# Fourteen weight pieces of the second convolution move from GpSimd in the scan to VectorE beside two attentions

## The chip, the cores and the metric

The kernel runs on one core of a Trainium2 chip. The metric is the device time of one execution in microseconds; times are compared as medians of several runs, profiles show one execution. Engines: PE (TensorE, matmuls), DVE (VectorE), ACT (ScalarE), POOL (GpSimd) and SP, whose queue issues most of the DMA transfers.

## The reference

Two layers work on x of shape (4, 512, 32, 32), float32. Both take a group norm of their input and add their result to it.

```python
# layer 0: a selective state-space scan over L = 1024 tokens, d_inner = 1024, 16 states
xz = layernorm(tokens) @ W_in                     # xm, z
xs = silu(causal_conv4(xm))
proj = xs @ W_x                                   # dt (32), B (16), C (16)
dt = softplus(proj[:, :32] @ W_dt + b_dt)
h = exp(dt * A) * h + dt * x * B                  # per channel and state
y = sum_s(h * C) + xs * D
out = (y * silu(z)) @ W_out
# layer 1: position attention between two 3x3 convolutions
sp = softmax(center(x)^T top(x))                  # 1024 x 1024, over all its elements
x2 = x + sp @ conv3x3(x, w_bottom)
out = conv3x3(x2, w_out)
```

## The kernel before

Layer 0. Work is cut into units (b, e, h, s): image b (4, called batch here), a pair e of 128-channel blocks (4), a half h of the tokens (2) and a state s (16), so 128 units per image and 512 in all. In a unit, ACT makes exp(dt*A) (line 837), DVE scans twice (line 889), and the product with C and the sum over s follow. The product of dt*x with B is made in one of two ways, by the table B_ON_ACT: on ACT, which scales transposed rows (line 849, four instructions of 128x256), with PE transposing them back (line 875, eight 128x128 transposes); or on POOL (line 864, one instruction of 128x1024 with B broadcast by a DMA). The product with C is one POOL instruction of 128x1024 (line 911), or two of 128x512 on DVE (line 905) for the states in C_ON_DVE. PE sums over s by transposing matmuls (line 918).

The convolutions of layer 1 are Winograd convolutions, four rows by two columns of output at a time: six row taps by four column taps. Their transformed weights are computed in layer 0, in 16 pieces for each convolution (`transform`, line 1159 on): three loads of 192 KB, two scalings on ACT (lines 1177 and 1178), three additions of 128x768 (1185, 1191, 1195) and nine of 128x256 (1203 to 1205) on POOL, and twelve stores to DRAM, to ub (first convolution, w_bottom) or uo (second, w_out). All 32 pieces are steps that fill gaps.

The order of layer 0 is written out by a planner, `Plan`: each step has an engine, an expected duration and a priority (units counted along the scan), and of the steps that can start the one with the smallest priority goes first, within a window. Piece k has the priority -5 for the first 7 (t0) and then tg * (k - 7).

Layer 1. Per image: `scores` (PE: pt and psc, ACT copies them to the eight tiles st, DVE takes the maximum, ACT the exponential), `conv3` (24 loads of 1 MB of weights, uw, each for four matmuls of 128x512 into one PSUM tile m; DVE forms the input transforms rr and v and the outputs n and y, POOL helps), `attend` (eight groups of matmuls pat, each evicted by one DVE instruction into the image, line 1566) and a second `conv3`, whose result `finish` transposes back, adds to the loaded residual and stores. `norm` normalizes the next image. The order before is, for each image b: conv b, attention b, scores b+1, second conv o, finish. In the last image the second convolution's first input is computed chunk by chunk within the attention (`by_chunk`), and half of the transposes back come before the last matmuls (`last`).

In layer 1 the recording framework orders the instructions of each engine and frees buffers of a tag as their readers end. Tag v (16 KB per partition) has two buffers, for the v tiles and for x1t, the image that norm reads; tag u three, for the convolution's weights; PSUM pool ps three.

Of the kernel before, what the change touches and what calls it, by code (L numbers as in the profile page):

```python
# [8 lines left out]
F32 = mybir.dt.float32  # L9
AF = mybir.ActivationFunctionType  # L10
ALU = mybir.AluOpType
# [16 lines left out]
GS = 16  # L28


PRM = dict(pg=0.53, kt=2, ke=1, ka=-0.68, fl=0, fi=4.6, m0=48, n0=50.77, nl=2.05, c0=61.67, cg=6.03, p0=112, e0=6, eg=4.75, g0=78.98, gg=9.04, o0=13.03, og=5.23, dl=8.5, t0=7, tg=18.5, zl=11.5, f1=1.5)


class Buf:
# [137 lines left out]
def mamba_then_pab_kernel(  # L172
# [70 lines left out]

    NP6, NQ = 6, 4
    ub, uo = (
        [
            dram.tile([NP6, P, NCC, C], F32, tag=f"u_{n}_{q}", name=f"u_{n}_{q}")
# [30 lines left out]
    with ExitStack() as l0:  # L280
# [1014 lines left out]
    with ExitStack() as l1:  # L1295
# [104 lines left out]

        shape = [P, NCC, TI, WW + 2]

        def by_chunk(name, xg):

            e, f = (
                tp.tile(shape, F32, tag="rt", name=f"{n}_{name}", bufs=4) for n in "ef"
            )
            r = tp.tile([P, 2, *shape[1:]], F32, tag="rr", name=f"rr_{name}_1", bufs=1)
            v = xp.tile([P, NQ, 2, NCC, P], F32, tag="v", name=f"v_{name}_1", bufs=2)

            def chunk(c):
                rows = [xg[:, c, a : a + 4 * TI - 3 : 4, :] for a in range(5)]
                for t, a in ((e, 2), (f, 1)):
                    nc.scalar.activation(t[:, c], rows[a], AF.Copy, scale=-4.0)
                    nc.gpsimd.tensor_add(t[:, c], t[:, c], rows[a + 2])
                nc.vector.tensor_add(r[:, 0, c], e[:, c], f[:, c])
                nc.vector.tensor_sub(r[:, 1, c], e[:, c], f[:, c])
                x = [r[:, :, c, :, a : a + 2 * TJ - 1 : 2] for a in range(4)]
                vq = [
                    v[:, q, :, c].rearrange("p n (i j) -> p n i j", j=TJ) for q in range(NQ)  # L1420
                ]
                nc.vector.tensor_sub(vq[2], x[2], x[1])  # L1422
                nc.vector.tensor_add(vq[1], x[1], x[2])
                nc.vector.tensor_sub(vq[0], x[0], x[2])
                nc.vector.tensor_sub(vq[3], x[1], x[3])

            return v, chunk

        def conv3(name, xg, u, bias, first=None, late=None):

# [3 lines left out]
            def rows(a):  # L1434
                return xg[:, :, a : a + 4 * TI - 3 : 4, :]

            def tmp(n):
                return tp.tile(shape, F32, tag="rt", name=f"{n}_{name}", bufs=4)

            def flat(t):  # L1440
                return t.rearrange("p c i x -> p (c i x)")

            def inputs(pair):

                r = tp.tile([P, 2, *shape[1:]], F32, tag="rr", name=f"rr_{name}_{pair[0]}", bufs=1)
                r0, r1 = r[:, 0], r[:, 1]
                if pair == (1, 2):
                    e, f = tmp("e"), tmp("f")
                    nc.scalar.activation(e, rows(2), AF.Copy, scale=-4.0)
                    nc.scalar.activation(f, rows(1), AF.Copy, scale=-4.0)  # L1450
                    nc.gpsimd.tensor_add(e, e, rows(4))
                    nc.gpsimd.tensor_add(f, f, rows(3))
                    nc.vector.tensor_add(r0, e, f)
                    nc.vector.tensor_sub(r1, e, f)
                    return r
                if pair == (3, 4):
                    g, h = tmp("g"), tmp("h")
# [9 lines left out]
                k, l = tmp("k"), tmp("l")  # L1467
# [8 lines left out]
            kept = []  # L1476
            y = [None] * 4
            for pair in PAIRS:
                if first and pair == (1, 2):
                    v = first  # L1480
                else:
                    r = inputs(pair)

                    v = xp.tile([P, NQ, 2, NCC, P], F32, tag="v", name=f"v_{name}_{pair[0]}", bufs=2)
                    rv = r.rearrange("p n c i x -> p (n c i) x")
                    x = [rv[:, :, a : a + 2 * TJ - 1 : 2] for a in range(4)]
                    vq = [v[:, q].rearrange("p n c (i j) -> p (n c i) j", j=TJ) for q in range(NQ)]
                    nc.vector.tensor_sub(vq[2], x[2], x[1])
                    nc.vector.tensor_add(vq[1], x[1], x[2])
                    nc.vector.tensor_sub(vq[0], x[0], x[2])  # L1490
                    nc.vector.tensor_sub(vq[3], x[1], x[3])
                ns = []
                for k, p in enumerate(pair):
                    m = {}
# [51 lines left out]
        def attend(b, xg, st, rp, xb, between, chunk):  # L1546


            for k in range(NCC * NH):
# [48 lines left out]
        def finish(b, y):  # L1598

            for j in range(NCC):  # L1600
                o = load_sum(b, j, fp, "f4")
                for rr in range(2):
                    turn_back(b, j, o, y, rr)
                nc.scalar.dma_start(dst[b][:, j, :], o)
# [14 lines left out]
        xg = image[0]  # L1619
        st, rp = scores(0, xg)  # L1620
        for b in range(B):
            xb = conv3(f"b{b}", xg, ub, brow[0])
            after = norm(b + 1) if b + 1 < B else iter(())
            next(after, None)

            v, chunk = by_chunk(f"o{b}", xg) if b + 1 == B else (None, None)
            attend(b, xg, st, rp, xb, after, chunk)
            if b + 1 == B:
                last(b, xg, v)
                break  # L1630
            st, rp = scores(b + 1, image[b + 1])
            finish(b, conv3(f"o{b}", xg, uo, brow[1]))
            xg = image.get(b + 1)


# [55 lines left out]
```

## Time and profile before

| | us |
|---|---|
| median of 3 runs (3073.21 to 3087.27) | 3081.69 |
| the profiled execution | 3079.09 |
| its span | 3077.3 |
| busy PE | 2789.0 (91%) |
| busy DVE | 2290.1 (74%) |
| busy ACT | 1822.0 (59%) |
| busy POOL | 2125.4 (69%) |
| layer 0, by the trace | about 0 to 2045 |
| layer 1 | about 2045 to 3077 |

The first table of the profile page counts busy time over the whole span, which mixes two layers of very different work; the views by stretch, given further on, hold them apart. In a group of instructions the columns are: line, engine, operation, output and inputs with shapes and count, then busy time and mean ns of one, then the idle time just before them and what ended it. Busy time of PE counts overlapped matmuls once, so busy time over count can be smaller than the mean.

### The profile page before, as it was taken

The page shows a single profiled execution, that of the slowest core. Times are in us where ns is not written, and L with a number is a line of the kernel's source. Part 1 is how long each engine was busy: PE and PEld are TensorE (multiplying, and loading weights), DVE is VectorE, ACT ScalarE, POOL GpSimd, SP SyncE. Part 2 cuts the span into 40 slices and gives each one's busy share as a digit, 9 for nine tenths or more (in the row PEclk, how much of TensorE's full clock was granted, in tenths as well). Part 3 has the DMA queues.
Part 4 walks back from the last instruction along what each step waited for, and adds up shares of the span by engine and source line. Part 5 has one row for each costly group of instructions (what it writes and reads, how often), then busy time and mean ns, then how long its engine had stood idle before and what let it go on. Part 6 is the DMA issues. An engine that isn't in the chain of part 4 may idle for free.

```text
span 3077.3 us, 36921 instructions
## 1 busy us (share of the span) xinstructions
PE 2789.0 (91%) x11896; PEld 1669.4 (54%) x11896; DVE 2290.1 (74%) x2989; ACT 1822.0 (59%) x3300; POOL 2125.4 (69%) x1197
## 2 busy tenths in 40 slices
PE   6788789999889999888999968879999999999998
PEld 2556566566666666666666656644444444444444
DVE  4579999888999988989988879985285375346344
ACT  4679878898888888788898879941120030030000
POOL 6989888899978899978889999952151143134222
PEclk9899899999999999999999989999999999999999
DMA  6756455577645577745567654448178458628827
GB/s 183 219 171 210 142 158 155 174 233 241 210 139 173 179 222 239 237 128 162 164 189 222 213 159 140 134 121 319 43 266 316 155 175 317 245 85 312 302 86 260
DMA packets 404537, 600.07 MB, mean 195 GB/s; under 512 B 47192, under 2 KB 246104, under 8 KB 379768
## 3 DMA queue, kind: packets, MB, share of 16 engines
q1 hardware_dynamic: 395536, 583.18, 59.8%
q10 hardware_dynamic: 8648, 14.26, 1.3%
q8 instruction: 95, 1.56, 0.2%
q14 instruction: 98, 0.80, 0.1%
q0 software_dynamic: 160, 0.26, 0.0%
HBM read 500.60 MB, written 96.99 MB: 194 GB/s over the span
## 4 chain that ended last, share of the span: by engine, by line
PE 40%; DVE 12%; ACT 6%; DMA 4%; POOL 4%; issue 3%; SPq 0%; DVEq 0%; POOLq 0%; ACTq 0%
PE m_o L1503 10%; PE m_b L1503 8%; PE pat L1553 7%; DVE da L889 5%; PE y L918 3%; PE po L402 2%; PE psc L1380 2%; PE u L875 2%; DMA uw_b<-u_b 2%; POOL da L911 2%; DVE dbx L889 2%; DVE u L889 1%; PE pz L402 1%; PE pp L728 1%; ACT sc L849 1%
## 5 line engine op out<-in xcount | busy, mean ns | idle before, releaser
L911 POOL TENSOR_TENSOR da<-da,cbc 128x1024 f32<-128x1024 f32 x328 | 773.2, 2368 | 114.7 <-DVE da L889 53.1
L849 ACT ACTIVATE sc<-dtxt,bt_sb 128x256 f32<-128x256 f32 x1312 | 578.1, 499 | 99.3 <-PE u L875 98.5
L837 ACT ACTIVATE da<-dt,a_sb 128x512 f32<-128x512 f32 x656 | 454.1, 716 | 78.8 <-PE y L918 62.8
L864 POOL TENSOR_TENSOR dbx<-dtx,bbc 128x1024 f32<-128x1024 f32 x184 | 434.4, 2373 | 10.6 <-DVE carry_sb L894 4.6
L889 DVE TENSOR_TENSOR_SCAN da<-da,carry_sb,u 128x512 f32<-128x512 f32 x328 | 403.1, 1262 | 42.4 <-PE u L875 40.1
L918 PE MATMUL y<-ident,da 128*128 128x128 f32 x2624 | 366.6, 284 | 72.1 <-POOL da L911 69.9
L889 DVE TENSOR_TENSOR_SCAN da<-da,u 128x512 f32<-128x512 f32 x328 | 397.9, 1213 | 31.0 <-PE u L875 29.0
L875 PE MATMUL u<-ident,sc 128*128 128x128 f32 x2624 | 389.2, 282 | 23.5 <-DVE da L889 14.8
L918 PEld LDWEIGHTS y<-ident,da 128*128 128x128 f32 x2624 | 309.4, 146 | 180.6 <-POOL da L911 132.3
L875 PEld LDWEIGHTS u<-ident,sc 128*128 128x128 f32 x2624 | 314.2, 145 | 113.5 <-issue 34.2
L1503 PE MATMUL m_b<-uw_b,v_b 128*128 128x512 f32 x768 | 337.6, 596 | 17.5 <-issue 8.3
L1503 PE MATMUL m_o<-uw_o,v_o 128*128 128x512 f32 x768 | 334.1, 595 | 4.5 <-DVE v_o L1422 4.1
L402 PE MATMUL pxm<-xt,winc 128*128 128x341 f32 (+4 forms) x768 | 251.0, 470 | 21.7 <-DVE xs L661 10.5
L1503 PEld LDWEIGHTS m_b<-uw_b,v_b 128*128 128x128 f32 x768 | 143.4, 190 | 204.1 <-issue 187.1
L402 PE MATMUL pz<-xt,winc 128*128 128x512 f32 x512 | 244.8, 599 | 8.8 <-DMA winc<-in_w_in_dram 2.5
L837 ACT ACTIVATE u<-dt,a_sb 128x512 f32<-128x512 f32 x368 | 245.5, 681 | 11.9 <-DVE da L889 6.7
L1503 PEld LDWEIGHTS m_o<-uw_o,v_o 128*128 128x128 f32 x768 | 145.6, 191 | 190.2 <-issue 181.7
L918 PE MATMUL y<-ident,dbx 128*128 128x128 f32 x1472 | 215.4, 285 | 36.0 <-DVE dbx L905 24.7
L918 PEld LDWEIGHTS y<-ident,dbx 128*128 128x128 f32 x1472 | 175.7, 147 | 88.2 <-DVE dbx L905 25.8
L1553 PE MATMUL pat<-y_b,st 128*128 128x512 f32 x512 | 221.7, 593 | 0.1
L661 DVE SCALAR_TENSOR_TENSOR xs<-pxm,cw_sb,xs 128x341 f32<-128x341 f32 (+8 forms) x288 | 163.6, 569 | 60.6 <-ACT xs L652 53.6
L1511 ACT ACTIVATE e_b<-m_b 128x512 f32<-128x512 f32 x24 | 14.3, 596 | 316.4 <-PE m_b L1503 300.0
(220 smaller groups left out, 4315.4 us busy)
## 6 DMA issues: line engine op xcount, KB each, us to landing
cbc<-bcd SPq DMA_DIRECT2D x512, 256.0 KB, 3.6
uw_b<-u_b SPq DMA_DIRECT2D x96, 1024.0 KB, 5.1
uw_o<-u_o SPq DMA_DIRECT2D x96, 1024.0 KB, 4.9
bbc<-bcd SPq DMA_DIRECT2D x184, 256.0 KB, 3.9
u_b<-work SPq DMA_DIRECT2D x192, 128.0 KB, 3.0
u_o<-work SPq DMA_DIRECT2D x192, 128.0 KB, 3.4
winc<-in_w_in_dram SPq DMA_DIRECT2D x72, 256.0 KB, 3.7
szd<-sz SPq DMA_DIRECT2D x32, 512.0 KB, 4.0
```

The costliest lines, as they stand in the source:

```text
L402: lambda k=k, lhs=lhs, rhs=rhs: nc.tensor.matmul(p()[:, at : at + cols], lhs(), rhs(), start=(k == 0), stop=(k == n - 1)),
L661: nc.vector.scalar_tensor_tensor(u()[:, first:end], p()[:, first - k - at + before : n - k + before], cw[k], u()[:, first:end], ALU.mult, ...
L837: nc.scalar.activation(t, dt()[:, j], AF.Exp, scale=a_sb[:, at : at + 1])
L849: nc.scalar.activation(sc()[:, k], dtxt()[:, k], AF.Copy, scale=bt[:, at, s : s + 1])
L864: lambda: nc.gpsimd.tensor_mul(hc(), dtx(), b_bc().to_broadcast([P, 2, T])),
L875: nc.tensor.transpose(u()[:, k * P : (k + 1) * P], sc()[:, k, j, :], ident)
L889: nc.vector.tensor_tensor_scan(ht, *((hc()[:, j], u()) if on_act else (u(), hc()[:, j])), carry_sb[:, j, s : s + 1] if h else 0.0, ALU.mul ...
L911: lambda: nc.gpsimd.tensor_mul(hc(), hc(), c_bc().to_broadcast([P, 2, T])),
L918: nc.tensor.matmul(y[j]()[:, k, :], hc()[:, j, k * P : (k + 1) * P], ident, start=(s == 0 and k == 0), stop=(s == NS - 1 and k == NK - 1), ...
L1380: nc.tensor.matmul(pt, top[:, m * P : (m + 1) * P], center[:, h * T : (h + 1) * T], start=True, stop=True,)
L1503: nc.tensor.matmul(m[q], v[:, q, k, c, :], w[:, c, :], start=(c == 0), stop=(c == NCC - 1 and not extra),)
L1553: nc.tensor.matmul(pt, st[m][:, 2 * P * j + h : 2 * P * (j + 1) : 2], xb[m // 2][:, m % 2, :], start=(m == 0), stop=(m == NMC - 1),)
```

## The change

Sixteen pieces of the first convolution's weights and two of the second's stay in layer 0 on POOL (EARLY = 2; tg 42 instead of 18.5). The other fourteen pieces are made by a new function `piece`, on DVE, seven beside the attention of image 0 and seven beside that of image 1. A piece has three loads, six DVE instructions on 384 elements, three on 768, and four stores of 128x6x128. The images go in pairs, so that both attentions of the first pair come before any second convolution: conv b0, attention 0, scores 1, conv b1, attention 1, conv o0, conv o1, scores 2, conv b2, and so on. norm(2) is called inside conv o1. The first input of conv o of a pair is computed before the pair's second attention (`first_inputs`); `by_chunk` goes. The tile of a piece has the tag v, its result the tag u.

In layer 0, nine of sixteen B products are on ACT instead of ten (ten instead of eleven in the last batch), and in the last batch three C products are on DVE instead of two.

```diff
-PRM = dict(pg=0.53, ..., t0=7, tg=18.5, zl=11.5, f1=1.5)
+PRM = dict(pg=0.53, ..., t0=7, tg=42, zl=11.5, f1=1.5)
...
-    NP6, NQ = 6, 4
+    NP6, NQ, EARLY = 6, 4, 2
...
-        B_ON_ACT = [(0, 2, 4, 6, 7, 8, 10, 12, 14, 15)] * (B - 1) + [(0, 2, 3, 4, 6, 8, 10, 11, 12, 14, 15)]
-        C_ON_DVE = [(1, 5, 9, 13)] * (B - 1) + [(5, 13)]
+        B_ON_ACT = [(0, 2, 4, 6, 8, 10, 12, 14, 15)] * (B - 1) + [(0, 2, 4, 6, 7, 8, 10, 12, 14, 15)]
+        C_ON_DVE = [(1, 5, 9, 13)] * (B - 1) + [(3, 9, 13)]
...
-        for k in range(2 * NPC):
+        for k in range(NPC + EARLY):
             u, src = ((ub, w_bottom), (uo, w_out))[k // NPC]
             transform(u, src, k % NPC, -5 if k < PRM['t0'] else PRM['tg'] * (k - PRM['t0']))
...
+        def first_inputs(name, xg):
+            r = row_pair(name, 1)
+            ts = []
+            for n, a in (("e", 2), ("f", 1)):
+                t = tmp(n, name)
+                rows = [xg[:, :, k : k + 4 * TI - 3 : 4, :] for k in (a, a + 2)]
+                nc.scalar.activation(t, rows[0], AF.Copy, scale=-4.0)
+                nc.gpsimd.tensor_add(t, t, rows[1])
+                ts.append(t)
+            nc.vector.tensor_add(r[:, 0], *ts)
+            nc.vector.tensor_sub(r[:, 1], *ts)
+            return spread(name, 1, r)
+
+        def piece(k):
+            c, part = divmod(k, C // QC)
+            cs = slice(part * QC, (part + 1) * QC)
+            taps = w_out[c * P : (c + 1) * P, :, cs].rearrange("p (y x) o -> p y x o", y=3)
+            t = xp.tile([P, NQ, 2, NCC, P], F32, tag="v", name=f"w_{k}", bufs=2)
...
+            nc.sync.dma_start(g[:, 0], taps[:, 0])
+            nc.sync.dma_start(g[:, NP6 - 1], taps[:, 2])
+            nc.sync.dma_start(mid[:, 0], taps[:, 1])
...
+            dve.tensor_add(r[1], r[0], r[5])
+            stt(r[3], r[5], 4.0, r[0], ALU.mult, ALU.add)
+            dve.tensor_sub(r[2], r[1], m)
+            dve.tensor_add(r[1], r[1], m)
+            stt(r[4], m, -2.0, r[3], ALU.mult, ALU.add)
+            stt(r[3], m, 2.0, r[3], ALU.mult, ALU.add)
+            o = fp.tile([P, NCC, C], F32, tag="u", name=f"wo_{k}", bufs=3)
...
+            dve.tensor_add(o[:, 0], g[:, :, 0], g[:, :, 2])
+            dve.tensor_sub(o[:, 1], o[:, 0], g[:, :, 1])
+            dve.tensor_add(o[:, 0], o[:, 0], g[:, :, 1])
+            for q, part in enumerate((g[:, :, 0], o[:, 0], o[:, 1], g[:, :, 2])):
+                nc.sync.dma_start(uo[q].rearrange("n p c o -> p n c o")[:, :, c, cs], part)
...
-                if h and chunk:
-                    chunk(j)
+                for job in also[k : k + 1]:
+                    if job is not None:
+                        piece(job)
...
+        left = list(range(EARLY, NPC))
+        half = len(left) // 2
+        st, rp = scores(0, image[0])
+        for a in range(0, B, 2):
+            for b in (a, a + 1):
+                xb = conv3(f"b{b}", image[b], ub, brow[0])
+                also = [None] * (8 - half) + left[b * half : (b + 1) * half] if not a else []
+                after, v = iter(()), None
+                if b == a:
+                    after = norm(b + 1)
+                    next(after)
+                else:
+                    v = first_inputs(f"o{a}", image[a])
+                attend(b, image[b], st, rp, xb, after, also)
+                if b == a:
+                    st, rp = scores(b + 1, image[b + 1])
+            finish(a, conv3(f"o{a}", image[a], uo, brow[1], v))
+            if a + 2 == B:
+                last(a + 1, image[a + 1], None)
+                break
+            y = conv3(f"o{a + 1}", image[a + 1], uo, brow[1], mid=lambda: normed(a + 2))
+            finish(a + 1, y)
+            st, rp = scores(a + 2, image[a + 2])
```

More of the change, by code (lines that the diff above doesn't have):

```diff
@@ L28 @@
 GS = 16
-PRM = dict(pg=0.53, kt=2, ke=1, ka=-0.68, fl=0, fi=4.6, m0=48, n0=50.77, nl=2.05, c0=61.67, cg=6.03, p0=112, e0=6, eg=4.75, g0=78.98, gg=9.04, o0=13.03, og=5.23, dl=8.5, t0=7, tg=18.5, zl=11.5, f1=1.5)
+PRM = dict(pg=0.53, kt=2, ke=1, ka=-0.68, fl=0, fi=4.6, m0=48, n0=50.77, nl=2.05, c0=61.67, cg=6.03, p0=112, e0=6, eg=4.75, g0=78.98, gg=9.04, o0=13.03, og=5.23, dl=8.5, t0=7, tg=42, zl=11.5, f1=1.5)
 class Buf:
@@ L1401, in mamba_then_pab_kernel @@
         shape = [P, NCC, TI, WW + 2]
[L1403 to L1427, printed above, removed]
@@ L1429, in conv3, with spread @@
-        def conv3(name, xg, u, bias, first=None, late=None):
+        def spread(name, p, r):
+            v = xp.tile([P, NQ, 2, NCC, P], F32, tag="v", name=f"v_{name}_{p}", bufs=2)
+            rv = r.rearrange("p n c i x -> p (n c i) x")
+            x = [rv[:, :, a : a + 2 * TJ - 1 : 2] for a in range(4)]
+            vq = [v[:, q].rearrange("p n c (i j) -> p (n c i) j", j=TJ) for q in range(NQ)]
+            nc.vector.tensor_sub(vq[2], x[2], x[1])
+            nc.vector.tensor_add(vq[1], x[1], x[2])
+            nc.vector.tensor_sub(vq[0], x[0], x[2])
+            nc.vector.tensor_sub(vq[3], x[1], x[3])
+            return v
@@ new lines, in tmp, with row_pair @@
+        def tmp(n, name):
+            return tp.tile(shape, F32, tag="rt", name=f"{n}_{name}", bufs=4)
+        def row_pair(name, p):
+            return tp.tile([P, 2, *shape[1:]], F32, tag="rr", name=f"rr_{name}_{p}", bufs=1)
+        def first_inputs(name, xg):
[10 more added lines that the diff above has]
+            return spread(name, 1, r)
@@ new lines, in piece @@
+        def piece(k):
[3 more added lines that the diff above has]
+            t = xp.tile([P, NQ, 2, NCC, P], F32, tag="v", name=f"w_{k}", bufs=2)
+            t = t.rearrange("p q n c t -> p (q n c t)").rearrange("p (r o) -> p r o", o=QC)
+            g, mid = (t[:, a : a + n].rearrange("p (r x) o -> p r x o", x=3) for a, n in ((0, 3 * NP6), (3 * NP6, 3)))
+            nc.sync.dma_start(g[:, 0], taps[:, 0])
+            nc.sync.dma_start(g[:, NP6 - 1], taps[:, 2])
+            nc.sync.dma_start(mid[:, 0], taps[:, 1])
+            r = [g[:, n].rearrange("p x o -> p (x o)") for n in range(NP6)]
+            m = mid[:, 0].rearrange("p x o -> p (x o)")
+            stt, dve = nc.vector.scalar_tensor_tensor, nc.vector
+            dve.tensor_add(r[1], r[0], r[5])
[5 more added lines that the diff above has]
+            o = fp.tile([P, NCC, C], F32, tag="u", name=f"wo_{k}", bufs=3)
+            o = o.rearrange("p c o -> p (c o)").rearrange("p (q r o) -> p q r o", o=QC, r=8)[:, :, :NP6]
+            dve.tensor_add(o[:, 0], g[:, :, 0], g[:, :, 2])
[3 more added lines that the diff above has]
+                nc.sync.dma_start(uo[q].rearrange("n p c o -> p n c o")[:, :, c, cs], part)
@@ L1434, in rows, with conv3 @@
+        def conv3(name, xg, u, bias, first=None, late=None, mid=None):
             def rows(a):
                 return xg[:, :, a : a + 4 * TI - 3 : 4, :]
-            def tmp(n):
-                return tp.tile(shape, F32, tag="rt", name=f"{n}_{name}", bufs=4)
             def flat(t):
@@ L1443, in inputs @@
             def inputs(pair):
-                r = tp.tile([P, 2, *shape[1:]], F32, tag="rr", name=f"rr_{name}_{pair[0]}", bufs=1)
+                r = row_pair(name, pair[0])
                 r0, r1 = r[:, 0], r[:, 1]
[L1447 to L1455, printed above, removed]
                 if pair == (3, 4):
-                    g, h = tmp("g"), tmp("h")
+                    g, h = tmp("g", name), tmp("h", name)
                     nc.gpsimd.tensor_sub(g, rows(4), rows(2))
@@ L1466, in inputs @@
                 g, h = kept
-                k, l = tmp("k"), tmp("l")
+                k, l = tmp("k", name), tmp("l", name)
                 nc.gpsimd.tensor_sub(l, rows(0), rows(2))
@@ L1478, in conv3 @@
             for pair in PAIRS:
-                if first and pair == (1, 2):
-                    v = first
-                else:
[L1482 to L1491, printed above, removed]
+                if pair == (1, 2):
+                    v = first or first_inputs(name, xg)
+                    if mid:
+                        mid()
+                else:
+                    v = spread(name, pair[0], inputs(pair))
                 ns = []
@@ L1544, in conv3, with attend @@
             return y
-        def attend(b, xg, st, rp, xb, between, chunk):
+        def attend(b, xg, st, rp, xb, between, also):
             for k in range(NCC * NH):
@@ L1617, in last, with normed @@
                 (nc.scalar, nc.sync)[j % 2].dma_start(dst[b][:, j, :], o[j])
[L1619 to L1629, printed above, removed]
+        def normed(b):
+            for _ in norm(b):
+                pass
+        left = list(range(EARLY, NPC))
[17 more added lines that the diff above has]
+                last(a + 1, image[a + 1], None)
                 break
-            st, rp = scores(b + 1, image[b + 1])
-            finish(b, conv3(f"o{b}", xg, uo, brow[1]))
-            xg = image.get(b + 1)
+            y = conv3(f"o{a + 1}", image[a + 1], uo, brow[1], mid=lambda: normed(a + 2))
+            finish(a + 1, y)
+            st, rp = scores(a + 2, image[a + 2])
 def kernel(**inputs):
```

## The prediction

> **What bounds the kernel now.** I read the busy time by stretch first. The kernel has two layers: the scan (to 2045 us, four batches of images of 540, 465, 480 and 435 us) and the convolutions with attention (1032 us). Each row gives the busy time of every engine.
>
> ```profile
> core 0: us, PE busy (x) PEld busy (x) DVE busy (x) ACT busy (x) POOL busy (x), PEclk, DMA share, GB/s
> 100.00:640.00 540.00, 473.85 (x2472) 325.33 (x2473) 456.79 (x634) 449.95 (x812) 476.79 (x281) 0.95 0.59 176
> 640.00:1105.00 465.00, 420.74 (x2257) 288.21 (x2256) 423.83 (x580) 397.22 (x717) 423.30 (x237) 0.97 0.64 192
> 1105.00:1585.00 480.00, 432.25 (x2320) 298.18 (x2319) 432.68 (x593) 405.42 (x734) 428.47 (x237) 0.96 0.62 191
> 1585.00:2020.00 435.00, 376.78 (x2188) 269.03 (x2186) 379.99 (x480) 384.95 (x720) 416.88 (x216) 0.95 0.60 178
> 2045.00:3077.00 1032.00, 997.81 (x2403) 444.27 (x2401) 530.65 (x588) 136.13 (x244) 299.31 (x148) 0.99 0.61 218
> ```
>
> In the scan no engine is alone the bound: in the second and third batch PE, DVE and POOL are all busy for 90 to 91%; in the last POOL is ahead with 96%. In layer 1 PE is busy for 97%: what makes PE wait there is lost. The groups give the prices, the waits the way in which POOL holds PE.
>
> ```profile
> L864 POOL TENSOR_TENSOR dbx<-dtx,bbc 128x1024 f32<-128x1024 f32 x184 | 434.4, 2373 | 10.6 <-DVE carry_sb L894 4.6
> L849 ACT ACTIVATE sc<-dtxt,bt_sb 128x256 f32<-128x256 f32 x1312 | 578.1, 499 | 99.3 <-PE u L875 98.5
> L1203 POOL TENSOR_TENSOR work<-work 128x256 f32<-128x256 f32 x96 | 70.2, 732 | 0.0
> L1185 POOL TENSOR_TENSOR work<-work 128x768 f32<-128x768 f32 x32 | 58.3, 1822 | 28.8 <-ACT work L1177 27.4 <-DMA u_b<-work 0.9 <-POOL da L911 0.4
> ```
>
> ```profile
> PEld y L918 <- POOL da L911: 139.2, 145, 11.9
> PE y L918 <- POOL da L911: 66.5, 61, 4.2
> ```
>
> For layer 1 I read one attention in order of time: PE runs 55 us of matmuls without a pause, DVE has one eviction of 0.75 us per 6.9 us. What fills DVE's gap looks free, but the same stretch shows what a DVE tensor_tensor costs beside POOL (3.60 us, against 1.25 alone).
>
> ```profile
> 2189.04 0.75 DVE L1566 SCALAR_TENSOR_TENSOR xg<-pat,rz,xg 128x512 f32<-128x512 f32 x1 [6.11 <-PE pat L1553]
> 2230.40 3.60 DVE L1489 TENSOR_TENSOR v_o<-rr_o 128x1024 f32<-128x1024 f32 x1
> 2238.55 1.25 DVE L1491 TENSOR_TENSOR v_o<-rr_o 128x1024 f32<-128x1024 f32 x1
> ```
>
> And the transfers, with KB and us to landing:
>
> ```profile
> uw_o<-u_o SPq DMA_DIRECT2D x96, 1024.0 KB, 4.9
> u_o<-work SPq DMA_DIRECT2D x192, 128.0 KB, 3.4
> work<-in_w_out_dram SPq DMA_DIRECT2D x48, 192.0 KB, 4.3
> ```
>
> **Step 1: the scan.** A piece on POOL is 3 x 1.82 + 9 x 0.73 = 12.0 us; 14 go: -168 us. One more B product per 16 states on POOL: 8 groups x 4 batches = 32 x 2.37 = +76. In the last batch one more C product per group moves to DVE: -8 x 2.37 = -19 on POOL, +16 x 0.68 (L905) = +11 on DVE. POOL: -111 us. ACT: 32 x 4 x 0.50 = -64, and the pieces' two scalings -14. PE: 256 transposes fewer at 389.2/2624 = 0.148 us: -38. SP sends 32 loads of 256 KB more, and the 14 pieces' 42 loads and 168 stores less.
>
> By batch: pieces in the trace are 9.7, 6.8, 6.8 and 3.3 per batch; with the new spacing (42 instead of 18.5 units) about 5.8, 3, 3 and 1. This leaves, as the highest engine: first batch PE 464 (POOL 449), second DVE 424 (PE 411, POOL 397), third DVE 433 (PE 423, POOL 402), last DVE 391 (POOL 389). DVE is not relieved at all, so the gain depends on how full the highest engine gets once the others have air. Bounds from the rows: it stays at the share it has now (88, 91, 90%; last batch falling to 91), or rises to the best share seen (96% in the last batch; 91% for the first, which has the ramp). First: 0 to -31, I take -14. Second: 0 to -22, -11. Third: 0 to -28, -14. Last: -6 to -27, -16. Nothing names a nearer row, so these are the middles. Sum -55 (-6 to -106).
>
> **Step 2: pieces beside attention.** On DVE a piece is six rows of 384 and three of 768 elements; by size from 1.21 us per 1024 elements (L1488) 2.7 + 2.7, with starts 5.6 us; 14 pieces 78 us. The seven of one attention (39 us) fit under 55 us, if their data are there in time. Here the two attentions differ.
>
> *Image 0.* The pieces take the two buffers of tag v in turn, one of them only after norm(1) has read x1t. DVE has, after the first load (4.3): 39 + 8 evictions (6) + norm (3) + the next convolution's rows and v (2.5 + 4.9) = 60 us. POOL makes six 1088-element operations (2.3 to 2.9 us) in the same time; at 3.6 against 1.2 us for a tensor_tensor beside it I add 9: 69. PE comes to the first tile of conv b1 after 55.4 + 7.0 (pt) = 62.4 us; its weights stand in SP's queue behind the last piece's stores, so about 72: +10 (0, if POOL is out of the way, to 20).
>
> The Trainium skill, SBUF, section "Who interferes with whom", speaks against the move: a VectorE instruction with two SBUF inputs and a GpSimd instruction that reads SBUF exclude each other for the whole instruction. The 3.60 us row agrees. By the rule alone each of some six GpSimd operations could hold one VectorE instruction for up to its own length, which would make 15 us of the 9.
>
> *Image 1.* v_o0 (the next convolution's first input) is made before this attention, and keeps one buffer of v until conv o0. All seven pieces share the other: in SP's queue the loads of piece k+1 stand behind the stores of piece k and wait until those from its buffer have landed. So a piece is a chain: load 4.3, DVE 5.6, and the stores of its ends, issued 2.7 us before DVE is done; 384 KB each, by size above the 3.4 of a 128 KB store, about 4.5, so 1.8 beyond: 11.7 us per piece. The first load waits for conv b1's last matmul. 4.3 + 5.6 + 6 x 11.7 = 80 us, then the last column's store (2.5 more) and uw_o0 (4.9): PE can start conv o0 at 87.5, its attention ends at 55.4: +32. Bounds from the smallest and largest landing of such loads (2.6 to 8.9) and stores (1.8 to 7.2): 8.2 to 19 us per piece, +9 to +83; the medians are the nearest. Behind SP's waits stand the weights that are prefetched now. PE's own attention is not held: three PSUM buffers cover an eviction that is late by 14 us.
>
> **Step 3: the order of images.** scores(2) comes after finish(1), norm(2) inside conv o1: its x1t takes the buffer of the next v; 2 MB more load beside 1 MB per 3.4 us; room of 27 us; I take +2 (0 to 8). At the start of layer 1 PE idles 8.30 us until the first v_b is written, since one tile of conv b0 stands ahead of the score matmuls (psc); in the new order psc comes first and waits some 2 us for top and center: -6 (-8 to 0). At the last attention PE waits 4.09 us for v_o: v_o2 is ready long before, -4 (-4 to 0). The removed by_chunk work (DVE 1.0 us rows) hid beside PE: 0.
>
> **Sum.** -55 + 10 + 32 + 2 - 6 - 4 = -21. The profiled execution took 3079.1 us (span 3077.3), 0.1% below the median of 3081.7: **3058 us**, 0.8% below the median.
>
> **Rivals.** *VectorE bounds the scan (slower).* The freed POOL only idles, as DVE keeps 424 and 433 us at the same 91 and 90% share: the scan gives 9 (the last batch and a little of the first). 3079 - 9 + 34 = 3104. For it: DVE is the highest engine in both middle batches and gets no relief; the shares of three engines are equal now. Against: 139 us of PE weight loads and 66 us of matmuls wait for POOL's C product. It decides when the scan gains less than 16 us.
> *The two layers cancel (same).* The scan gives 40: 3073. Anything from 18 to 48 is within 0.5%, which is about what a measurement of this kernel can tell from no change.
> *The pieces hide entirely (faster still).* Stores and loads overlap better, both attentions stay covered: 3079 - 55 - 8 = 3016. Against: the single buffer in the second attention; seven serial loads of 2.6 us and 5.6 us of work are 57 us already.
>
> **How the numbers follow.** My forecast 0.38 (its own range 3035 to 3066), hidden entirely 0.09, cancelled 0.23, VectorE bound 0.30. Faster 0.47, same 0.23, slower 0.30. The range runs from the hidden case to just past the slower one, 3018 to 3106; beyond lie the chain at its longest landing times and a scan at its best share.
>
> **What would show it.** In the changed profile: layer 0 ends near 1990 instead of 2045 us; POOL's share in the middle batches falls to 86 to 88%, DVE's rises to 93% or more. In the second attention loads of w come about every 12 us, and PE idles some 30 us between the last pat and the first m_o. At the end PE goes from pat to m_o without the 4.09 us. Wrong it would be with layer 0 above 2030 us (DVE bound), or with w loads every 8 us and no gap on PE.

## The result: the changed kernel is slower, and the profile after

| | before | after |
|---|---|---|
| median of 4 runs, us | 3079.46 | 3103.67 |
| ratio | | 1.0077 (95% interval 1.0054 to 1.0099) |
| profiled execution, span, us | 3077.3 | 3101.7 |
| scan, first dtx to last yt, us | 1942.0 | 1926.4 |
| last yt to first psc, us | 27.4 | 22.3 |
| first psc to the end, us | 1015.9 | 1059.7 |

The forecast was 3058 us, faster; the kernel lost 24 us. The lower half of the table shows where, and is read from the first or last instruction of a tile in the two traces: dtx opens a group of 16 units, yt closes one, psc is the first matmul of layer 1's scores. The scan and its tail gained 19 us (15.6 and 5.1, less a start 1.3 us later), layer 1 lost 44.

Per batch (the stretch, its length, and the time that each engine was busy in it), with the end of a batch put at its last yt, first the kernel before and then the one after:

```profile
core 0: us, PE busy (x) PEld busy (x) DVE busy (x) ACT busy (x) POOL busy (x), PEclk, DMA share, GB/s
92.00:689.60 597.60, 521.48 (x2731) 359.40 (x2730) 504.57 (x709) 499.24 (x902) 531.41 (x309) 0.95 0.62 182
689.60:1168.90 479.30, 434.89 (x2359) 298.58 (x2358) 439.17 (x599) 412.60 (x750) 437.76 (x245) 0.98 0.65 194
1168.90:1656.80 487.90, 441.16 (x2368) 304.53 (x2366) 436.44 (x595) 415.97 (x754) 437.92 (x243) 0.96 0.62 190
1656.80:2034.10 377.30, 318.68 (x1859) 228.17 (x1858) 330.83 (x413) 317.41 (x591) 353.18 (x182) 0.95 0.56 165
```

```profile
core 0: us, PE busy (x) PEld busy (x) DVE busy (x) ACT busy (x) POOL busy (x), PEclk, DMA share, GB/s
93.30:689.60 596.30, 517.98 (x2660) 355.13 (x2659) 503.58 (x709) 481.32 (x857) 503.32 (x267) 0.94 0.58 170
689.60:1177.30 487.70, 432.51 (x2294) 292.66 (x2293) 438.94 (x599) 397.47 (x709) 409.71 (x204) 0.97 0.59 178
1177.30:1661.00 483.70, 433.63 (x2298) 295.41 (x2297) 437.55 (x597) 397.41 (x711) 408.49 (x204) 0.96 0.60 179
1661.00:2019.70 358.70, 309.70 (x1803) 220.80 (x1802) 336.75 (x425) 307.43 (x562) 329.79 (x158) 0.97 0.59 168
```

What was to be taken off was taken off: in the middle batches GpSimd (POOL) has 28 and 29 us less to do, ScalarE (ACT) 15 and 19. The batches are 8.4 longer and 4.2 us shorter. VectorE (DVE) has the same 439 and 437 us. Only the last batch, where GpSimd was clearly the fullest engine (94%, the next, VectorE, 88%), is much shorter, by 18.6 us; VectorE is the fullest there now, with 94%.

The wait that spoke for a gain is the second thing to look at. From the list of waits of the whole span (us in total, times, longest), before and then after:

```profile
PEld y L918 <- POOL da L911: 144.5, 150, 11.9
PE y L918 <- POOL da L911: 69.9, 65, 4.2
POOL da L911 <- DVE da L889: 53.1, 30, 4.6
PEld y L918 <- POOL dbx L911: 21.8, 29, 2.2
PE y L918 <- POOL dbx L911: 10.4, 12, 1.9
```

```profile
PEld y L918 <- POOL da L911: 132.4, 140, 5.4
PE y L918 <- POOL da L911: 73.2, 48, 5.1
POOL da L911 <- DVE da L889: 70.4, 37, 5.0
PEld y L918 <- POOL dbx L911: 32.9, 49, 2.8
PE y L918 <- POOL dbx L911: 15.7, 16, 2.1
```

The C product stands in two tiles: da where B was multiplied on ScalarE, dbx where it was multiplied on GpSimd, and in the first three batches the new tables move one state per group from the first to the second. Over both, TensorE waits for GpSimd's C product as long as before (247 us before, 254 after), though GpSimd lost 109 us of work in the scan. What grew is GpSimd's own wait for VectorE's scan. So the wait reads as the last link of a chain (scan on VectorE, 2.37 us product on GpSimd, sum on TensorE), not as a queue of work on GpSimd.

Layer 1 is read from TensorE's waits, from 2020 us on. The longest in the kernel before:

```profile
PE m_b L1503 <- issue: 8.3, 1, 8.3
PE m_b L1503 <- DMA uw_b<-u_b: 8.3, 12, 1.4
PE m_o L1503 <- DVE v_o L1422: 4.1, 1, 4.1
PE psc L1380 <- ACT top L1371: 3.8, 3, 1.3
```

In the changed kernel:

```profile
PE m_o L1518 <- DMA uw_o<-u_o: 35.9, 1, 35.9
PE m_b L1518 <- DMA uw_b<-u_b: 9.4, 5, 4.3
PE pm_l L1334 <- DVE mv_l L1328: 7.2, 1, 7.2
PE pt L1359 <- DVE xg L1581: 4.5, 1, 4.5
```

The 35.9 us stand ahead of conv o0, behind the second attention. Its chain, in the order of time (start, us, what), shows the single buffer:

```profile
2326.89 4.11 DMA w<-in_w_out_dram
...
2335.12 3.78 DMA u_o<-w
2339.38 4.08 DMA w<-in_w_out_dram
...
2346.92 3.78 DMA u_o<-w
2351.17 4.09 DMA w<-in_w_out_dram
```

A load, VectorE's work on it, its stores, and only then the next load: one piece per 12 us, while TensorE's eight groups of pat were through at 2371.0. The first matmul of conv o0 came at 2406.9:

```profile
2406.90 5.53 PE L1518 MATMUL m_o<-uw_o,v_o 128*128 128x512 f32 x7 [35.90 <-DMA uw_o<-u_o]
```

Seven matmuls took 5.53 us there; near the end of the same convolution seventeen took 7.46 us without a pause ahead of them (from 2485.61 us). So the pause costs a little more than itself. The granted clock was 0.71 in the 64 us from 2368 on, where it was 1.00 in the kernel before. The Trainium skill, TensorE: Matmul & The Clock Gate, section Part 1: The HAM clock gate, says that the clock is halved after an idle window of about 3.4 us and comes back after a busy one of that length; the 5.53 us agree in direction.

In the first attention two chains meet, VectorE's pieces and GpSimd's row operations. VectorE's lines of one piece and GpSimd's beside them:

```profile
2156.32 2.42 DVE L1449 TENSOR_TENSOR w<-w 128x384 f32<-128x384 f32 x1 [0.17 <-DMA w<-in_w_out_dram]
2158.66 2.65 DVE L1450 SCALAR_TENSOR_TENSOR w<-w 128x384 f32<-128x384 f32 x1
2161.23 0.74 DVE L1581 SCALAR_TENSOR_TENSOR xg<-pat,rz,xg 128x512 f32<-128x512 f32 x1
2161.89 2.23 DVE L1451 TENSOR_TENSOR w<-w 128x384 f32<-128x384 f32 x1
2164.05 0.55 DVE L1453 SCALAR_TENSOR_TENSOR w<-w 128x384 f32<-128x384 f32 x1
```

```profile
2155.29 3.03 POOL L1429 TENSOR_TENSOR e_b<-e_b,xg 128x1088 f32<-128x1088 f32 x1
2158.29 2.60 POOL L1429 TENSOR_TENSOR f_b<-f_b,xg 128x1088 f32<-128x1088 f32 x1
2160.86 2.85 POOL L1481 TENSOR_TENSOR h_b<-xg 128x1088 f32<-128x1088 f32 x1
```

An instruction of 0.55 us takes 2.2 to 2.7 us: it ends within half a microsecond after the GpSimd instruction beside it. The eviction, which reads PSUM, keeps its 0.74 us. When GpSimd is through, at 2163.7, the 0.55 us are back. Six VectorE instructions are held in this attention, 11.6 us in all over what they take alone.

### The profile page after: what moved, and what is told of

The parts are those of the page before. It is cut to its first block, busy times and chain, and to the rows that moved or that the text cites. A ratio compares the mean times of both kernels' runs of the same rounds, so it can differ in the third digit from the quotient of the medians.

```text
span 3101.7 us, 36068 instructions
## 1 busy us (share of the span) xinstructions
PE 2772.7 (89%) x11640; PEld 1648.9 (53%) x11640; DVE 2370.7 (76%) x3113; ACT 1759.5 (57%) x3137; POOL 2020.5 (65%) x1047
## 4 chain that ended last, share of the span: by engine, by line
PE 40%; DVE 19%; ACT 6%; DMA 5%; issue 3%; POOL 2%; SPq 0%; ACTq 0%; DVEq 0%; POOLq 0%
PE m_o L1518 10%; PE m_b L1518 10%; DVE da L889 6%; PE pat L1568 4%; PE y L918 3%; PE po L402 3%; DVE dbx L889 2%; DVE u L889 2%; PE u L875 2%; PE pz L402 2%; DVE xs L661 2%; ACT sc L849 2%; PE psc L1380 2%; DMA w<-in_w_out_dram 1%; ACT da L837 1%
## 5 line engine op out<-in xcount | busy, mean ns | idle before, releaser
L911 POOL TENSOR_TENSOR da<-da,cbc 128x1024 f32<-128x1024 f32 x296 | 698.0, 2364 | 141.7 <-DVE da L889 70.4
L849 ACT ACTIVATE sc<-dtxt,bt_sb 128x256 f32<-128x256 f32 x1184 | 521.4, 499 | 128.2 <-PE u L875 127.4
L864 POOL TENSOR_TENSOR dbx<-dtx,bbc 128x1024 f32<-128x1024 f32 x216 | 509.8, 2367 | 69.2 <-PE y L918 44.7
L837 ACT ACTIVATE da<-dt,a_sb 128x512 f32<-128x512 f32 x592 | 409.5, 715 | 59.2 <-PE y L918 50.4
L918 PE MATMUL y<-ident,da 128*128 128x128 f32 x2368 | 330.2, 284 | 77.6 <-POOL da L911 73.2
L889 DVE TENSOR_TENSOR_SCAN da<-da,carry_sb,u 128x512 f32<-128x512 f32 x296 | 363.3, 1260 | 25.6 <-PE u L875 24.9
L889 DVE TENSOR_TENSOR_SCAN da<-da,u 128x512 f32<-128x512 f32 x296 | 358.7, 1212 | 22.7 <-PE u L875 22.7
L1518 PE MATMUL m_o<-uw_o,v_o 128*128 128x512 f32 x768 | 337.5, 600 | 35.9 <-DMA uw_o<-u_o 35.9
L837 ACT ACTIVATE u<-dt,a_sb 128x512 f32<-128x512 f32 x432 | 287.1, 681 | 33.7 <-DVE da L889 17.2
L918 PE MATMUL y<-ident,dbx 128*128 128x128 f32 x1728 | 253.5, 286 | 30.9 <-POOL dbx L911 15.7
L402 PE MATMUL pxm<-xt,winc 128*128 128x341 f32 (+4 forms) x768 | 255.1, 474 | 24.4 <-DVE xs L661 8.6
L911 POOL TENSOR_TENSOR dbx<-dbx,cbc 128x1024 f32<-128x1024 f32 x96 | 226.9, 2364 | 27.0 <-DVE carry_sb L894 14.5
```

Of the source, the lines that this page charges most:

```text
L402: lambda k=k, lhs=lhs, rhs=rhs: nc.tensor.matmul(p()[:, at : at + cols], lhs(), rhs(), start=(k == 0), stop=(k == n - 1)),
L837: nc.scalar.activation(t, dt()[:, j], AF.Exp, scale=a_sb[:, at : at + 1])
L849: nc.scalar.activation(sc()[:, k], dtxt()[:, k], AF.Copy, scale=bt[:, at, s : s + 1])
L864: lambda: nc.gpsimd.tensor_mul(hc(), dtx(), b_bc().to_broadcast([P, 2, T])),
L889: nc.vector.tensor_tensor_scan(ht, *((hc()[:, j], u()) if on_act else (u(), hc()[:, j])), carry_sb[:, j, s : s + 1] if h else 0.0, ALU.mul ...
L911: lambda: nc.gpsimd.tensor_mul(hc(), hc(), c_bc().to_broadcast([P, 2, T])),
```

## The experiments

Two theories stood at the start. The first is the slower rival of the prediction: VectorE bounds the scan, so freeing GpSimd frees nothing. The second: the tables eat the gain; one more B product per 16 states on GpSimd costs what the pieces gave. "Scan" below is the time from the first dtx to the last yt in the profiled execution: 1942.0 us before, 1926.4 after. Its scatter is read from kernels whose scans are alike: 1942.0, 1940.4 and 1934.4 with the tables and pieces of before, 1926.4, 1927.7 and 1927.0 with those of the changed kernel. It belongs to one execution, and where that execution was far from the median of its run the text says by how much.

**The order of the images alone**

```diff
-    NP6, NQ, EARLY = 6, 4, 2
+    NP6, NQ, EARLY = 6, 4, 16
```

with tg 18.5 and both tables as before.

> The images stay in pairs, but all 32 weight pieces are made in the scan, at the spacing and with the tables of the kernel before; nothing lies beside the attentions. This prices the order of the images alone. The scan should end where it ended before (last group of y starts at about 1988 us). Both theories (VectorE bounds the scan; the tables eat the gain) expect the same: the new start of layer 1 -6, norm(2) inside conv o1 +7 as the changed kernel's trace showed, the last attention -4, no gap of 8.9 us after the first attention and none of 35.9 us after the second: 3076 us, within 0.3% of the kernel before.

3067.4 us, ratio 0.9960 (0.9945 to 0.9975). The new order is a gain by itself, 9 us more than expected: the 4.1 us ahead of the last m_o are gone as expected, and the waits for uw_b are 2.4 us, against 8.3 before, which I had not counted. The 8.3 us at the start of layer 1, which I had put down to the order of the images, are still there:

```profile
PE m_b L1518 <- DVE v_b L1409: 8.3, 1, 8.3
PE pm_l L1334 <- DVE mv_l L1328: 6.5, 1, 6.5
PE m_b L1518 <- DMA uw_b<-u_b: 2.4, 3, 1.1
```

**The tables of before in the changed kernel**

```diff
-        B_ON_ACT = [(0, 2, 4, 6, 8, 10, 12, 14, 15)] * (B - 1) + ...
+        B_ON_ACT = [(0, 2, 4, 6, 7, 8, 10, 12, 14, 15)] * (B - 1) + [(0, 2, 3, 4, 6, 8, 10, 11, 12, 14, 15)]
-        C_ON_DVE = ... + [(3, 9, 13)]
+        C_ON_DVE = ... + [(5, 13)]
```

> The changed kernel with the two tables of the kernel before: the 14 pieces are gone from the scan, and no product is moved to GpSimd in exchange. Theory 'VectorE bounds the scan': VectorE's work in the first three batches is the same in all three kernels, so the scan stays within 15 us of the changed kernel's (3089 to 3104 us); GpSimd's share in the middle batches falls to about 81%, and what it gains is idle time. Theory 'the tables eat the gain' (one more B product per group on GpSimd costs what the pieces gave): the scan ends 25 to 45 us earlier than the changed kernel's, 3060 to 3078 us.

3097.6 us, scan 1925.9 against 1926.4, and GpSimd's share in the middle batches is 81%. The second of them:

```profile
687.90:1173.00 485.10, 441.64 (x2359) 303.09 (x2357) 439.13 (x599) 410.52 (x742) 391.90 (x196) 0.96 0.57 175
```

The 8.3 us at the start of layer 1 are back. The profiled execution took 10.8 us more than the median. By the medians this run is 6 us faster than the changed kernel in spite of that start, which leaves some 12 us to the scan. So the tables eat between nothing and 12 us, not the 25 to 45 of the second theory, which falls: without the pieces, and with no product moved, the scan is 16 us shorter than before by the profile, 27 at the most. GpSimd, with 163 us less to do, waits 169 us for VectorE's scan and the copy of its last column (carry_sb), 73 before.

**Two buffers in the second attention**

```diff
+                if k == 6 and between_end:
+                    between_end()
...
-                also = [None] * (8 - half) + left[b * half : (b + 1) * half] if not a else []
+                also = [None] * (8 - half) * (1 - b) + left[b * half : (b + 1) * half] if not a else []
...
-                    v = first_inputs(f"o{a}", image[a])
+                made = lambda: v.append(first_inputs(f"o{a}", image[a]))
```

> The changed kernel, but in the second attention conv o0's first v is made after the seventh piece instead of before the first, so that the pieces take both buffers of v in turn, and they start one slot earlier. If the single buffer is what stretches the pieces to one per 12 us, the loads come about every 7 us and the idle time of TensorE ahead of conv o0 falls from 35.9 us to 5 to 15 us: 3074 to 3084 us, level with the kernel before. If the rate of the transfers stretches them, the gap stays above 28 us and the time above 3095 us.

3072.54 us (0.9962 to 0.9982), and the wait ahead of conv o0 is 6.4 us:

```profile
2377.73 7.50 PE L1518 MATMUL m_o<-uw_o,v_o 128*128 128x512 f32 x13 [6.38 <-DMA uw_o<-u_o]
```

The rate of the transfers, the rival named, is excluded: the gap went with the way the buffers are used. Two things changed together, though. The first piece is now worked on ahead of the attention (VectorE begins it at 2301.0 us, with the first pat at 2316.0; before the edit at 2319.1), and the other six follow faster: not at the 7 us expected but in twos, 17.5 us apart. Both need the second buffer free, but the pieces were also put one slot earlier, and the share of that is not separated.

**One C product per group from VectorE to GpSimd**

```diff
-        C_ON_DVE = [(1, 5, 9, 13)] * (B - 1) + [(3, 9, 13)]
+        C_ON_DVE = [(3, 9, 13)] * B
```

> The changed kernel with three instead of four C products per group on VectorE in the first three batches, so that VectorE has 10.9 us less per batch and GpSimd 19 us more. Theory 'VectorE bounds the scan': the three batches gain up to 10 us each, 3070 to 3094 us. Theory 'GpSimd still bounds it' (the tables eat the gain): 10 to 19 us lost per batch, 3130 us or more. If neither is the bound and the changeovers between groups are, the time stays within 8 us of the changed kernel's 3104 us.

3107.96 us, scan 1936.4: 25 us less on VectorE and 56 more on GpSimd make 10 us more (4 of them may be the execution, which was that far above the median). Neither engine is the bound of the whole scan. I formed a new theory from a table that I worked out from the traces: the busy share of each engine in % in twelve equal parts of a group, from its first sum on TensorE (y) to the first of the next group, mean of the 16 groups of the middle batches.

```
before  DVE   95  98  96  91  96  86  75  74  98  94  88  97
        ACT   96  87  46  61  81  77  96  96  97  94  94  98
        POOL  90  90  94  92  95  87  78  88  98  89  94  89
        PE    94  84  80  87  96  95  90  83  94  98  93  91
after   DVE   93  98  95  91  84  80  80  83  93  96  88  95
        ACT   96  79  41  67  80  82  92  96  86  73  85  97
        POOL  80  81  77  63  83  82  81  95  98  85  91  91
        PE    93  78  81  90  91  87  91  83  94  99  99  82
```

In each part but one (the sixth of after) some engine is at 91% or more, and it isn't always the same one. GpSimd's share fell most in the first five parts, where VectorE or TensorE are at 91% or more. The theory: the bound changes within each group. Four runs took about as much work off one engine at a time in the changed kernel.

```diff
# VectorE: its C products        # GpSimd: C product for s in (4, 12)
-                if on_dve:
-                    step("DVE", 0.6, ...)
-            if not on_dve:
+            if not on_dve and s not in (4, 12):
                 step("POOL", 2.31, ...)
# TensorE: sum over the same states that VectorE multiplies
+                if not on_dve:
                     step("PE", 4 * TR, add, ...)
# ScalarE: B product for s in (4, 12)
+                    if s not in (4, 12):
                         step("ACT", ROWS, rows, ...)
```

> The changed kernel, but the C products that VectorE makes (four of 16 states per group, three in the last batch) are left out, and their loads with them: TensorE adds the scanned states without the product. VectorE loses 64 x 0.68 = 43 us per batch (32 in the last), nothing goes to another engine. The changed kernel's scan, from the first dtx to the last y, took 1926 us. Theory 'VectorE bounds the scan': it shortens by 110 to 160 us. Theory 'the bound changes within each group' (VectorE at its start, ScalarE and TensorE after it, GpSimd near its end, each full in turn): by 50 to 90 us, since VectorE is at 93% or more in about half of a group. If neither, and the order of the queues sets it: under 30 us.

> The changed kernel, but GpSimd's C product is left out for states 4 and 12 of each group, and its load: 16 x 2.37 = 38 us less on GpSimd per batch, and in two of 16 units a step less between VectorE's scan and TensorE. Theory 'VectorE bounds the scan': under 15 us shorter in all four batches. Theory 'the bound changes within each group': 0 to 40 us. If the number of units in flight sets it (a unit's way through the engines, not their load), two of 16 units are shorter by 2.4 us, about 2% of the way: under 40 us as well.

> The changed kernel, but ScalarE's B product is left out for states 4 and 12 of each group: TensorE turns the unscaled dtx back. ScalarE loses 64 x 0.50 = 32 us per batch. Theory 'VectorE bounds the scan': under 15 us shorter. Theory 'the bound changes within each group': 20 to 50 us, since ScalarE is at 94% or more in about a third of a group although its mean share is 81%.

> The changed kernel, but the products of the same four (last batch three) states are not added to y: TensorE loses 256 transposes per batch, 36 us by 0.143 us each; what VectorE makes of them is read by nobody. Theory 'VectorE bounds the scan': under 15 us shorter. Theory 'the bound changes within each group': 25 to 60 us. If TensorE alone were the bound: 110 to 145 us.

| work left out in the changed kernel | us less on it, count by mean | busy time, us | scan, us | change | time, us |
|---|---|---|---|---|---|
| VectorE | 161 | -138 | 1852.4 | -74 | 3025.62 |
| GpSimd | 152 | -147 | 1898.7 | -28 | 3067.09 |
| ScalarE | 128 | -97 | 1914.7 | -12 | 3087.20 |
| TensorE | 135 | -49 | 1937.0 | +11 | 3103.78 |

Busy time in the scan fell by less than the count by the mean, since it counts overlapping instructions once. VectorE and GpSimd came out as the new theory had it; ScalarE gave less (-12 also fits the theory that VectorE bounds the scan), and TensorE nothing at all. The +11 is one execution, 9.6 us above the median of its run; the median is that of the changed kernel. Leaving out a product does more than free its engine: with it go one step of a unit's way, on VectorE and GpSimd the load of 256 KB (more loads on VectorE's side), and on VectorE the tile u is free earlier. These were not separated, so the slopes are those of the whole edit. The second batch of the kernel with less on TensorE has a reason in its row:

```profile
691.90:1177.40 485.50, 409.75 (x2006) 268.49 (x2005) 436.09 (x596) 396.89 (x705) 407.19 (x204) 0.93 0.57 175
```

It has 288 matmuls fewer than the changed kernel's second batch, but a granted clock of 0.93 instead of 0.97: of the 41 us that they took (0.143 us each), busy time shows 23. All four executions of this run had a lower clock, 0.942 to 0.949 over the whole program against 0.960 to 0.965 in the changed kernel's, and in the scan of the two profiles the 2368 transposes of u, the same in both, took 291 ns in the mean instead of 283.

The same two subtractions in the kernel before tell whether VectorE was the stronger lever there already.

> The kernel before with VectorE's C products left out, and their loads (four states per group, two in the last batch): 151 us less on VectorE in the whole scan, which took 1942 us from the first dtx to the last yt. If VectorE was the stronger lever in the kernel before already: 55 to 85 us shorter, as in the changed kernel (74 of 161). If GpSimd, then at 90 to 96%, held the scan: under 30 us.

> The kernel before with GpSimd's C product left out for states 4 and 12 of each group, and its load: 152 us less on GpSimd. If VectorE was the stronger lever already: 10 to 35 us shorter (28 of 152 in the changed kernel). If GpSimd held the scan: 50 to 110 us.

Scan 1879.1 and 1907.3 us, times 3020.5 and 3038.49. Against the mean of the three like scans, 1939, that is 60 us for 151 of VectorE and 32 for 152 of GpSimd. VectorE was the stronger lever before the change; a microsecond taken off GpSimd gave 0.2, one off VectorE 0.4. The chain shows here too: without VectorE's products TensorE waits 194 us for GpSimd's C product instead of 247, with GpSimd's work unchanged.

**The tables with all pieces in the scan**

The kernel before with the tables of the changed kernel.

> The kernel before with the two tables of the changed kernel; all 32 pieces stay in the scan. GpSimd has 57 us more in all, ScalarE 64 less, TensorE 38 less, VectorE 11 more. Theory 'the bound changes within each group', with the slopes that the four runs with work left out gave (us of scan per us of work: VectorE 0.46, GpSimd 0.18, ScalarE 0.09, TensorE none): +10 - 6 + 5 = +9, 3088 us (3082 to 3096). If GpSimd, already at 90 to 96%, becomes the only bound: up to +57, above 3115 us.

3102.27 us, scan 1973.5: 35 us above the mean of the like scans, not 9 (the execution was 4.7 us above the median). The slopes do not add up over such steps: with GpSimd at 92% of the middle batches (456.94 of 499.20 us in the second) 57 us more cost 30 to 35. So the tables cost that with the pieces in the scan, and 0 to 12 us without them. The start of layer 1 has no wait of 8.3 us in this run, though the images keep their old order: it goes with the tables. Not with them alone: the kernel before with GpSimd's products left out keeps its tables and has no such wait either (psc at 2021.0 us, the first m_b at 2034.8). Which of the two comes first follows from how the last batch is planned.

**Towards a better kernel**

norm(2) later in conv o1, on the two runs that had been faster than before:

```diff
                     ns.append(n)
+                    if mid and p == 1:
+                        mid()
```

> The run with the images in pairs and all pieces in the scan (3067 us), with one more edit: norm(2) is begun after the first of the eight stages of conv o1 instead of ahead of it. If its 6.5 us of idle TensorE come from VectorE's queue, where the statistics stand behind an addition that waits for a load, they lie under matmuls now: 3061 us (3056 to 3066). If the first v of the next stage is what comes late instead, as norm's buffer is the next v's, the wait only moves: 3065 to 3070 us.

> The run with two buffers for the pieces of the second attention (3072.5 us), with norm(2) begun later in conv o1 as well: 7 us less, 3065 us (3060 to 3070); 3070 to 3075 us if the wait only moves.

3065.28 us (0.9947 to 0.9974) and 3066.61 us (0.9952 to 0.9976), 2 and 6 us below the runs that they change. The wait for mv_l (6.5 and 7.2 us) went, and one for the weights uw_o of 5.2 and 4.8 us came in nearly the same place: most of it only moved, and the rest of the 6 us is not explained.

Seven pieces beside the attentions and nine of uo in the scan (tg 26, the first input made after the pieces, norm(2) later), first with the new tables, then with ten B products on ScalarE in all batches:

```diff
-    NP6, NQ, EARLY = 6, 4, 2
+    NP6, NQ, EARLY = 6, 4, 9
...
+        also = [[None, None, 9, None, 10, None, 11], [12, None, 13, None, 14, None, 15]][b] if not a else []
...
-        B_ON_ACT = [(0, 2, 4, 6, 8, 10, 12, 14, 15)] * (B - 1) + [(0, 2, 4, 6, 7, 8, 10, 12, 14, 15)]
+        B_ON_ACT = [(0, 2, 4, 6, 7, 8, 10, 12, 14, 15)] * B
```

> The changed kernel with seven pieces beside the attentions instead of 14 (three in the first, four in the second, two buffers, every second slot), nine of the second convolution's in the scan at an even spacing, and norm(2) begun later. Theory 'the bound changes within each group', with the slopes measured: the seven pieces cost the scan 84 x 0.18 = 15 us, so layer 1 starts at about 2057 us (2042 in the changed kernel); of the 22 us of waits in layer 1 of the run with two buffers about 5 to 10 are left: 3058 to 3068 us. If GpSimd's load doesn't matter at all in the scan, 3045 to 3053 us; if it counts in full, above 3080 us.

> The run with seven pieces beside the attentions (3071 us), but with ten B products on ScalarE in all batches: the tables of the kernel before in the first three batches, those of the changed one in the last. If the new tables of the first three batches cost time wherever pieces are in the scan, the scan falls from 1956 to 1920 to 1935 us, and the time to 3050 us (3042 to 3058). If the tables don't matter: 3065 to 3078 us.

> All pieces in the scan, images in pairs, norm(2) begun later (3065 us), with the tables of the changed kernel in the last batch alone. In the kernels with that last table TensorE begins layer 1 with the score matmuls and has no idle time of 8.3 us there: 3055 us (3050 to 3062) if that is kept, 3062 to 3070 us if not.

3071.4 us, above the 3058 to 3068 expected (scan 1955.6, in an execution 8.8 us above the median); 3055.97 us, ratio 0.9929 (0.9915 to 0.9943), scan 1939.6; and 3063.11 us (0.9940 to 0.9968), scan 1942.0 with all pieces in it. The middle run is the fastest of those that do all the work, faster than both kernels. Its time is in the range expected, but its scan, as long as the like scans of before, is not; its gain is layer 1 and its start, where little is left to wait for:

```profile
PE m_o L1516 <- DMA uw_o<-u_o: 4.8, 3, 3.6
PE m_b L1516 <- DMA uw_b<-u_b: 3.4, 3, 2.1
PE m_o L1516 <- DVE n_o L1532: 1.3, 1, 1.3
PE psc L1380 <- issue: 1.3, 1, 1.3
```

In the last run the 8.3 us are gone too, with the last batch's table alone; its time is only 2 us below the run that differs from it by that table (3065.28), with a scan 8 us longer in the profiled execution, which is the scatter of like scans.

## Why the prediction was wrong

| step | forecast, us | measured, us |
|---|---|---|
| 1, scan: first batch | -14 | -1.3 |
| second | -11 | +8.4 |
| third | -14 | -4.2 |
| last | -16 | -18.6 |
| 2, image 0 | +10 | +8.8 (4.5 and 4.3) |
| 2, image 1 | +32 | +35.9 |
| 3, norm(2) in conv o1 | +2 | +7.2 |
| 3, start of layer 1 | -6 | -5.1 |
| 3, last attention | -4 | -4.1 |
| sum of layer 1's terms | +34 | +42.7 |
| span | -21 | +24.4 |

The measured terms leave +1.3 us for the later start of the scan and -4 us for the other waits of layer 1. The measured batches end at their last yt, those of the forecast at 640, 1105, 1585 and 2020 us, so single batches compare roughly, and their sum exactly: -55 forecast, -15.7 measured.

**Step 1 failed**, and it decides the sign: 39 of the 45 us between forecast and result. The step said that the gain "depends on how full the highest engine gets once the others have air", and took the middle between the share of now and the best share seen. The share did not rise, and that it would was the part without a reason: VectorE filled 92 and 89% of the middle batches before, and 90 and 90% after, where 93% or more was to show. Layer 1 began at 2042 us; above 2030 had been named as the mark of a wrong forecast. The runs with work left out show what relief of GpSimd is worth instead: of work taken from it in the kernel before, a fifth shows in the scan, and the pieces, which only fill gaps, were worth 16 to 27 of 168 us under the old tables. The last batch, the one stage where GpSimd was clearly ahead, is the one where the term was right, and its mechanism too: VectorE, then the fullest, went from 88 to 94%. One bound was off by the step's own rule as well: in the first batch 464 us at the share of now, 88%, give -13 and not 0. That moves the middle of that batch to -22 and makes the forecast worse. The ends of the four ranges add to -108, not -106.

The row I read against the rival, 139 us of weight loads that wait for GpSimd's C product, was misread. It fell by 12 us of 144.5 over the whole span, and the same wait in the tile dbx rose by 11. TensorE's waits for the product in both tiles, 247 us before, were still 229 with the old tables and 163 us off GpSimd, and 194 in the kernel before without VectorE's products. So its releaser is better read as the last link of a chain that begins at VectorE.

The slower rival gave 3104 us for 3103.5, and its place was right: VectorE kept its work, the freed GpSimd idled. Its name was too strong, though. VectorE does not bound the scan alone: 25 us less of it with 56 more on GpSimd brought nothing, and GpSimd's 152 us are worth 28. That each group has several bounds in turn fits the two strongest slopes; ScalarE's and TensorE's were smaller than that theory asked, and the 35 us of the tables with all pieces were more than the slopes gave. What sets the scan's time in each part of a group is not settled. The planner's order changes with every edit, and was not held fixed in any run.

**Step 2 held.** Image 1 by its mechanism and size: one buffer, 12 us a piece, 35.9 us for the 32; two buffers, with the pieces one slot earlier, took 30 of them away. Image 0: 8.8 for 10, 4.3 of it the weights behind the stores, as the step had it, and 4.5 a late eviction ahead of pt, which it had not named; that the sum fits is partly luck. GpSimd held VectorE's instructions for 11.6 us, where the row of 3.60 us had given 9. The estimate of 15 us by the Trainium skill (SBUF, Who interferes with whom) was the one too high, but its exclusion is what the lines show: an instruction with two SBUF inputs lasts until the GpSimd one ends.

**Step 3**: norm(2) was under-sized, 7.2 for 2, inside its range of 0 to 8. The room of 27 us was there for the data, but not in VectorE's queue: the last statistics stood behind an addition that waited for a load, 7.75 us, and a matmul waited for them at the head of TensorE's queue.

```profile
2511.46 1.41 DVE L1610 TENSOR_TENSOR o<-o,po 128x256 f32<-128x256 f32 x4 [7.75 <-DMA o<-x]
```

The start of layer 1 came out as forecast by luck, for a wrong reason: not the order of the images but the new plan of the last batch, which goes with the tables, brings psc ahead of m_b0. The last attention was right.

## What to carry to other kernels

Here three engines were at 90%, and taking work from one of them gave a fraction of it that could not be read from shares. Leave out a tenth of one engine's work at a time and measure the slope before moving anything, and do not stretch the slope to a larger step. A wait names the last link: ask whether that engine was busy with something else (a queue) or was itself waiting (a chain), since in this kernel relief of the last link did not shorten a chain. And before work is put beside a stage that has free engine time, count the buffers that it can turn over, and set them against load, work and store in a row.

## What the runs showed of the hardware that I had not expected

Less work on TensorE bought nothing, and its granted clock went from 0.97 to 0.93 in the second batch: with 13% fewer matmuls it was busy for only 5% less time (432.51 to 409.75 us). It was lower as well in the stretch with the 36 us pause ahead of conv o0 (0.71 in those 64 us, 1.00 before). In this kernel time freed on TensorE was partly paid back by its clock.
